# Two layers of attention and gated network on one core: the first layer's bank of sums copied in two halves, by ScalarE and VectorE

## The chip, the core and the metric

The kernel runs on one core of a Trainium2 chip. The time is the device time of one execution in microseconds, and the lower the better. Everything is computed in float32. A core has TensorE (PE in the profile; PEld is its weight load), VectorE (DVE), ScalarE (ACT), GpSimd (POOL) and SyncE (SP, which here only starts DMA transfers). Each engine works through a queue of its own in order. TensorE writes its products into banks of 128 partitions x 512 numbers; ScalarE and VectorE read them from there into the large on-chip memory, and from there DMA transfers take them.

## The reference

Two layers over 2048 tokens of 128 numbers. Each is `x = x + s * silu(f)`, where s is an attention of the normalised x and f a second network of it. The change lies in the attention of the first layer, which has no softmax: a query's weights are the rectified scores, divided by their sum.

```python
def kernel_func(q, k):
    scores = jnp.einsum('bhqd,bhkd->bhqk', q, k) / jnp.sqrt(jnp.asarray(HD, q.dtype))
    w = jax.nn.relu(scores)
    return w / (jnp.sum(w, axis=-1, keepdims=True) + KERN_EPS)
...
attn = kernel_func(q, k)
out = jnp.einsum('bhqk,bhkd->bhqd', attn, v)
out = out.transpose(0, 2, 1, 3).reshape(Bx, Sx, D)
out = out @ w_out + b_out
y = x + out
mu = jnp.mean(y, axis=-1, keepdims=True)
var = jnp.var(y, axis=-1, keepdims=True)
return (y - mu) * jax.lax.rsqrt(var + LN_EPS) * gamma + beta
```

It has 16 heads of 8 numbers and all 2048 keys for each query. The first layer's second network (the routed block) picks 255 tokens by a score, runs a small transformer block on them and puts them back. The second layer has a causal softmax attention of 16 heads of 64 and a gated network; nothing of it is changed.

## The kernel before

`relu_attention` is written as 256 steps. A step n stands for a quarter of the queries (qc, 512 of them), a group of four heads (g) and a block of 128 keys (kb): qc = n // 64, g = n // 16 % 4, kb = n % 16. So 16 steps make a group, and there are 16 groups.

`scores(n)` issues four matmuls (L994), one for each head of the group, each into one of six banks that are used in turn (tag "s"). Each result is rectified and scaled into a tile `rt` by ScalarE (L1002) or by VectorE (L1004). `Work.lesser` (L191) chooses: it keeps a running count of booked time for both engines and gives the piece to the one whose count would be lower. Other pieces that are put on either engine are booked with `work.add`.

`products(m, r)` runs two steps behind the scores: four matmuls (L1010, eight instructions in the profile) multiply the rectified scores with the values. They add up over a group's 16 steps in one bank, `acc`, in which head j has the partitions 32j to 32j + 8 (eight numbers and the sum of the weights). The first step of a group starts the bank afresh.

After the 16th step of a group `group_out` (L1017) copies all 128 x 512 numbers of `acc` into a tile `part` (L1026), one of two in turn, and books 0.6 for ScalarE. Then five DMA transfers take the sums (L1028) and the four heads' rows (L1031) out of `part`. When a quarter of the queries has its four groups, `gated` (L1033) divides, multiplies by the output weights, normalises and applies the gate; it is cut into pieces by `yield`.

PE, ScalarE and VectorE follow the written order. In the main loop (L1143) a step issues: the scores and their rectifiers of step n; a `later` left over from the step before; the products of step n - 2 and, where that was a group's last, `group_out`; then one piece of other work (the routed block's, the second network's weights, or `gated`'s); and at some steps DMA loads of keys and queries. So on ScalarE the copy stands behind the rectifiers of step n, and before the other work of step n and the rectifiers of step n + 1. On PE the scores of step n + 1 stand between the last products of one group and the first of the next, which have to wait until the bank has been copied.

The tile framework sets the waits between the engines: an instruction waits for what it reads, and for those that still use what it overwrites.

Of the kernel before, what the change touches and what calls it, by code (L numbers as in the profile page):

```python
# [16 lines left out]
AF = mybir.ActivationFunctionType  # L17
ALU = mybir.AluOpType
# [88 lines left out]
def layer0(ctx, tc, a, small, ident, xin, xsrc, xn1T, row_load, second):  # L107
# [33 lines left out]
    for n, bit in (("k", 2), ("q", 1)):  # L141
# [30 lines left out]
        row_load, (b_out, gamma, beta, xin),  # L172
    )
    relu_attention(
        tc, work, at, aw, end, dram, small, ps, ident, (w_q, w_k, w_qa, w_ka, w_v), lows, w_out, xin, xne,
        xnT, g0, xn1T, routed, (ends, steps, block), second,
# [589 lines left out]
def relu_attention(  # L766
# [3 lines left out]
    nc = tc.nc  # L770
    scale = 1.0 / math.sqrt(HD0)
# [11 lines left out]
    def bank(shape, tag="x"):  # L783
        return ps.tile(shape, F32, tag=tag, bufs=NS if tag == "s" else 1, name="t")
# [26 lines left out]
    def query_tile(qc, g):  # L811
        t = qTs[qc, g] = aw.tile([P, 512], F32R, tag="qT", bufs=3, name=f"qT_{qc}_{g}")
        return t
# [26 lines left out]
    def group(parts, order, g, dst):  # L840

        for n, x in enumerate(order):
            nc.sync.dma_start(out=dst.bitcast(F32)[n::4, :], in_=parts[x][32 * g : 32 * g + 32, :])
# [4 lines left out]
    def key_group(parts, i, g):  # L848
        group(parts, OF_K, g, kT[:, g, 512 * i : 512 * i + 512])
# [135 lines left out]
    acc = bank([P, 512], "acc")  # L985
    nc.vector.memset(acc, 0.0)

    def scores(n):
        qc, g, kb = n // 64, n // 16 % 4, n % 16
        r = []  # L990
        for j in range(4):
            rows = slice(32 * j, 32 * j + 32)
            t = bank([P, 512], "s")
            nc.tensor.matmul(  # L994
                t, kT[rows, g, kb * P : (kb + 1) * P], qTs[qc, g][rows, :],
                start=True, stop=True,
            )
            rt = aw.tile([P, 512], F32, tag="relu", bufs=12, name="rt")
            r.append((rt, t))
        for rt, t in r:  # L1000
            if work.lesser(512):
                nc.scalar.activation(rt, t, AF.Relu, scale=scale)  # L1002
            else:
                nc.vector.tensor_scalar(rt, t, scale, 0.0, ALU.mult, ALU.max)  # L1004
        return [rt for rt, _ in r]

    def products(n, r):
        g, kb = n // 16 % 4, n % 16
        for j in range(4):
            nc.tensor.matmul(  # L1010
                acc[32 * j : 32 * j + HD0 + 1, :], va[:, kb, 4 * g + j, :], r[j],
                start=(kb == 0), stop=(kb == NC - 1),
            )
# [3 lines left out]
    def group_out(qc, g):  # L1017

        if g == 0:
            got[qc] = [  # L1020
                end.tile([P, 512], F32, tag="on", bufs=3, name=f"on_{qc}"),
                small.tile([P, 64], F32, tag="sums", name=f"sums_{qc}"),
            ]
        on, sums = got[qc]
        part = end.tile([P, 512], F32, tag="part", bufs=2, name="part")
        nc.scalar.copy(part, acc)  # L1026
        work.add(a=0.6)
        nc.sync.dma_start(out=sums[32 * g : 32 * g + 32, :], in_=part[HD0::32, :])  # L1028
        for j in range(4):
            r0 = HD0 * (4 * g + j)  # L1030
            nc.sync.dma_start(out=on[r0 : r0 + HD0, :], in_=part[32 * j : 32 * j + HD0, :])  # L1031
# [94 lines left out]
    def others():  # L1126
        yield from routed
        block.close()
        yield from second.ffn_weights(
            ends.enter_context(tc.tile_pool(name="l1_f", bufs=1, side="right")), work  # L1130
        )
        for qc in range(NQ):
            while qc not in ready:
                yield
            yield from gated(qc)

    ends, steps, block = pools
    ready, held, other, later = set(), [], others(), None
# [4 lines left out]
    for n in range(n_steps + 2):  # L1143
        if n == 16:
            first.close()
        if n < n_steps:
            held.append((n, scores(n)))
        if later:
            later()
            later = None  # L1150
        if n >= 2:
            m, r = held.pop(0)
            products(m, r)
            if m % 16 == 15:
                group_out(m // 64, m // 16 % 4)
        if n in due:
            f, *args = due[n]
            later = f(*args)
        else:
            next(other)  # L1160
        if n in read:
            i, g = read[n]
            key_group(key_rows[i], i, g)
        if n == 11 or (n > 16 and n % 16 == 8 and n + 8 < n_steps):
            m = 16 if n == 11 else n + 8
            qc, g = m // 64, m // 16 % 4
            group(asked[qc], OF_Q, g, query_tile(qc, g))

        if n >= 2 and (n - 2) % 64 == 6 and n > 64:
            ready.add((n - 2) // 64 - 1)  # L1170
# [4 lines left out]
    early = second.early()  # L1175
# [785 lines left out]
```

## Time and profile before

| what | us |
|---|---|
| three runs: lowest, median, highest | 1429.67, 1430.36, 1430.63 |
| the profiled execution, its own time | 1430.62 |
| its span, first instruction to last | 1428.8 |
| the first layer's 256 steps, first products at 18.2 to last at 471.5 | 453 |
| copies of the bank (L1026), 16 of 605 ns | 9.7 |
| rectifiers on ScalarE (L1002), 595 of 606 ns | 315.3 |
| rectifiers on VectorE (L1004), 429 of 684 ns | 276.8 |
| scores on TensorE (L994), 1024 matmuls, time in which any of them runs | 155.9 |
| products on TensorE (L1010), 2048 instructions, time in which any of them runs | 267.4 |

In the stretch from 300 to 400 us TensorE is busy for 98.8 us, VectorE for 84.2 and ScalarE for 83.2; the granted clock of TensorE is 1.00.

How to read the profile's lines. A group of instructions gives the line of the kernel, the engine, the operation, result <- operands by the program's names, the shapes and the count; then the busy time in us, the mean ns of one; then the idle time of the engine just before them and what ended it. `t` is the name that the profile gives to every bank of the first layer, `acc` among them. A line of a timeline gives the start in us from the span's start, the duration in us, and the same names; instructions of one kind that follow each other are drawn together (x8), and the bracket is the idle time of the engine before the first.

### The profile page before, as it was taken

Reading aid. Unit: us, or ns where it says so; the run is one execution under the profiler, and the core shown is the slowest. Engines: PE = TensorE matmul, PEld = TensorE weight load, DVE = VectorE, ACT = ScalarE, POOL = GpSimd, SP = SyncE. Lnnn points to the kernel's source line nnn. Section 1 sums busy time; section 2 is a strip of 40 time slices with the busy share of each in tenths; the row PEclk is TensorE's granted clock in tenths of the full one; section 3 lists DMA queues with packets and bytes.
Section 4 is the critical chain, followed back from the end, with each engine's and each line's share of the span. In section 5 each row is a group of like instructions: output and inputs, shape, how many; then the busy total and the mean of one; then the engine's idle time right before and its main releaser. Section 6 shows DMA issues by size and latency. Waiting matters only on the chain.

```text
span 1428.8 us, 26989 instructions
## 1 busy us (share of the span) xinstructions
PE 1394.9 (98%) x10112; PEld 850.7 (60%) x10112; DVE 1061.3 (74%) x1930; ACT 953.1 (67%) x2054; POOL 307.5 (22%) x414
## 2 busy tenths in 40 slices
PE   8999999999999999999999999999999999999997
PEld 4222332322222477777777777777777777777775
DVE  7688788788888486668668678668768768777775
ACT  5588877788888566666557556566566656656563
POOL 3001000150000131322323232242242233242210
PEclk9999999999999999999999999999999999999999
DMA  3632001101000310111111101111011111111110
GB/s 95 170 78 63 12 13 36 47 27 44 19 20 5 101 38 23 31 31 45 31 28 33 45 16 46 31 31 45 17 45 37 25 31 46 31 31 31 30 38 16
DMA packets 44082, 56.48 MB, mean 40 GB/s; under 512 B 11696, under 2 KB 26416, under 8 KB 43952
## 3 DMA queue, kind: packets, MB, share of 16 engines
q1 hardware_dynamic: 43568, 53.70, 14.7%
q8 instruction: 80, 1.31, 0.4%
q0 software_dynamic: 384, 1.05, 0.3%
q14 instruction: 50, 0.41, 0.1%
HBM read 27.74 MB, written 8.35 MB: 25 GB/s over the span
## 4 chain that ended last, share of the span: by engine, by line
PE 62%; ACT 1%; DVE 1%; issue 0%; DVEq 0%; ACTq 0%
PE t L1520 18%; PE z L1570 18%; PE t L1791 16%; PE m L1671 2%; PE m L1473 2%; PE m L1458 2%; PE m L1423 2%; ACT p L1554 1%; PE m L1352 0%; ACT pt L1798 0%; PE m L1370 0%; DVE tops L1541 0%; DVE zs L1654 0%; DVE res L1689 0%; ACT L1361 0%
## 5 line engine op out<-in xcount | busy, mean ns | idle before, releaser
L1541 DVE TENSOR_REDUCE tops<-t 128x1 f32<-128x1024 f32 (+4 forms) x320 | 334.5, 1062 | 94.7 <-PE t L1520 88.1
L1002 ACT ACTIVATE rt<-t 128x512 f32<-128x512 f32 x595 | 315.3, 606 | 67.8 <-PE t L994 66.5
L1798 ACT COPY pt<-t 128x512 f32<-128x512 f32 (+3 forms) x359 | 163.4, 519 | 262.1 <-PE t L1791 260.9
L1554 ACT ACTIVATE p<-t,tops 128x1024 f32<-128x1024 f32 (+7 forms) x384 | 330.9, 882 | 1.3 <-DVE tops L1541 1.1
L1004 DVE TENSOR_SCALAR rt<-t 128x512 f32<-128x512 f32 x429 | 276.8, 684 | 64.4 <-PE t L994 59.9
L1520 PE MATMUL t<-k,q 128*128 128x512 f32 (+4 forms) x1280 | 312.9, 387 | 3.7 <-ACT p L1554 3.7
L1791 PE MATMUL t<-ident,p 128*128 128x128 f32 x2176 | 270.0, 275 | 2.9 <-ACT x L1444 1.4
L1010 PE MATMUL t<-rt,va 128*9 128x512 f32 x2048 | 267.4, 595 | 4.7 <-ACT part L1026 4.7
L1570 PE MATMUL z<-pt,v 128*64 128x256 f32 (+1 forms) x2304 | 268.4, 374 | 0.5 <-ACT zs L1805 0.5
L1520 PEld LDWEIGHTS t<-k,q 128*128 128x128 f32 x1280 | 217.9, 189 | 77.0 <-issue 32.2
L1791 PEld LDWEIGHTS t<-ident,p 128*128 128x128 f32 x2176 | 243.5, 141 | 25.4 <-ACT pt L1798 5.7
L1570 PEld LDWEIGHTS z<-pt,v 128*64 128x64 f32 x2304 | 152.1, 137 | 86.6 <-issue 22.8
L994 PEld LDWEIGHTS t<-qT,kT 32*128 32x128 f32 x1024 | 65.3, 182 | 181.5 <-ACT rt L1002 99.1
L1798 DVE COPY pt<-t 128x512 f32<-128x512 f32 (+3 forms) x289 | 163.6, 605 | 3.9 <-PE z L1570 2.0
L994 PE MATMUL t<-qT,kT 32*128 32x512 f32 x1024 | 155.9, 496 | 2.8 <-DMA kT<-spread 1.3
L1446 POOL CAST q<-x 64x512 fp32r<-64x512 f32 x60 | 36.5, 609 | 454.5 <-ACT x L1444 452.8
L1540 DVE TENSOR_TENSOR t<-t,mask_q 128x128 f32<-128x128 f32 (+1 forms) x192 | 64.7, 337 | 74.9 <-PE t L1520 68.5
L1554 ACT ACTIVATION_READ_ACCUMULATOR p<-t,tops 128x1 f32 x384 | 84.3, 220 | 0.0
L1448 POOL TENSOR_TENSOR k<-x,k 64x512 fp32r<-64x512 f32 x60 | 76.4, 1273 | 4.6
L1448 POOL TENSOR_TENSOR q<-x,q 64x512 fp32r<-64x512 f32 x60 | 76.2, 1270 | 4.6
L1010 PEld LDWEIGHTS t<-rt,va 128*9 128x9 f32 x2048 | 30.8, 89 | 69.2 <-issue 60.2
L1446 POOL CAST k<-x 64x512 fp32r<-64x512 f32 x60 | 38.3, 639 | 128.6 <-ACT x L1444 126.8
(330 smaller groups left out, 938.1 us busy)
## 6 DMA issues: line engine op xcount, KB each, us to landing
q<-q SPq DMA_DIRECT2D x64, 256.0 KB
wide<-rows SPq DMA_DIRECT2D x90, 128.0 KB
qT<-spread SPq DMA_DIRECT2D x60, 64.0 KB
kT<-spread SPq DMA_DIRECT2D x48, 64.0 KB
spread<-high SPq DMA_DIRECT2D x8, 256.0 KB
spread<-low SPq DMA_DIRECT2D x8, 256.0 KB
rows<-xne SPq DMA_DIRECT2D x1, 1048.0 KB
back<-nothing SPq DMA_DIRECT2D x4, 256.0 KB
```

The costliest lines, as they stand in the source:

```text
L994: nc.tensor.matmul(t, kT[rows, g, kb * P : (kb + 1) * P], qTs[qc, g][rows, :], start=True, stop=True,)
L1002: nc.scalar.activation(rt, t, AF.Relu, scale=scale)
L1004: nc.vector.tensor_scalar(rt, t, scale, 0.0, ALU.mult, ALU.max)
L1010: nc.tensor.matmul(acc[32 * j : 32 * j + HD0 + 1, :], va[:, kb, 4 * g + j, :], r[j], start=(kb == 0), stop=(kb == NC - 1),)
L1446: nc.gpsimd.tensor_copy(high, x[half(e), :])
L1448: nc.gpsimd.tensor_tensor(low, x[half(e), :], high, ALU.subtract)
L1520: nc.tensor.matmul(flat[:, at_x : at_x + y - x], q[:, part, c4 * P : (c4 + 1) * P], k[:, x:y], start=(part == 0), stop=(part == 1),)
L1541: nc.vector.tensor_reduce(M[pr, c // 4][:, h, c % 4, es], x, axes, ALU.max, negate=True)
L1554: nc.scalar.activation(dst, x, AF.Exp, bias=M[pr, c // 4][:, h, c % 4, e : e + 1], accum_out=Z[pr, c // 4][:, h, c % 4, e : e + 1],)
L1570: nc.tensor.matmul(l1.z[half(e), slot, lo:2, :], V[pr, h][:, kb, half(e)], pts[e][:, kb, lo:2, :], start=(kb == 0), stop=(kb >= n0 - 1), s ...
L1791: nc.tensor.transpose(t[:, k + b, :], x[lo + b], ident)
L1798: copy(dst, t)
```

## The change

`group_out` copies the columns 0 to 255 of the bank by ScalarE and the columns 256 to 511 by VectorE, one after the other in the written order, and books 0.4 for each. `scores` returns, besides its tiles, a function that rectifies those of the four results that it hasn't rectified itself; the loop calls it after the products. How many it rectifies itself is given by the loop, and it is 4 in both branches.

```diff
-    def scores(n):
+    def scores(n, early=4):
...
-        for rt, t in r:
-            if work.lesser(512):
-                nc.scalar.activation(rt, t, AF.Relu, scale=scale)
-            else:
-                nc.vector.tensor_scalar(rt, t, scale, 0.0, ALU.mult, ALU.max)
-        return [rt for rt, _ in r]
+
+        def rectified(some):
+            for rt, t in some:
+                if work.lesser(512):
+                    nc.scalar.activation(rt, t, AF.Relu, scale=scale)
+                else:
+                    nc.vector.tensor_scalar(rt, t, scale, 0.0, ALU.mult, ALU.max)
+
+        rectified(r[:early])
+        return [rt for rt, _ in r], lambda: rectified(r[early:])
...
         part = end.tile([P, 512], F32, tag="part", bufs=2, name="part")
-        nc.scalar.copy(part, acc)
-        work.add(a=0.6)
+
+        nc.scalar.copy(part[:, :256], acc[:, :256])
+        nc.vector.tensor_copy(part[:, 256:], acc[:, 256:])
+        work.add(a=0.4, d=0.4)
...
+        rest = None
         if n < n_steps:
-            held.append((n, scores(n)))
+
+            rows, rest = scores(n, 4 if n % 16 == 1 and n > 16 else 4)
+            held.append((n, rows))
...
+        if rest:
+            rest()
```

## The prediction

> **What bounds the kernel now.** I read the page first (busy shares, then the costliest groups), then the copy's own line, then the timeline at one end of a group, then looked for a place where ScalarE and VectorE already read one bank.
>
> ```profile
> PE 1394.9 (98%) x10112; PEld 850.7 (60%) x10112; DVE 1061.3 (74%) x1930; ACT 953.1 (67%) x2054; POOL 307.5 (22%) x414
> ...
> L1010 PE MATMUL t<-rt,va 128*9 128x512 f32 x2048 | 267.4, 595 | 4.7 <-ACT part L1026 4.7
> ```
>
> TensorE is busy for 98% of the span. Where it stands idle in the products of the first layer, the only releaser named is the copy of the bank, 4.7 us in all. The copy's own line says how often:
>
> ```profile
> L1026 ACT COPY part<-t x16: 585/600/651, 60.7 to 472.2; 128x512 f32<-128x512 f32 x16
> ...
>   PEld t L1010: 9.0, 14
>   PE t L1010: 4.7, 12
> ```
>
> So 12 of the 16 copies leave TensorE idle, 0.27 to 0.48 us each. The timeline shows how, at the end of the seventh group:
>
> ```profile
> 243.77 1.05 PE L1010 MATMUL t<-rt,va 128*9 128x512 f32 x8
> ...
> 243.96 2.60 DVE L1004 TENSOR_SCALAR rt<-t 128x512 f32<-128x512 f32 x4
> ...
> 244.74 0.50 PE L994 MATMUL t<-qT,kT 32*128 32x512 f32 x4
> 244.88 0.58 ACT L1026 COPY part<-t 128x512 f32<-128x512 f32 x1
> ...
> 245.52 1.04 PE L1010 MATMUL t<-rt,va 128*9 128x512 f32 x8 [0.27 <-ACT part L1026]
> ...
> 246.93 1.05 PE L1010 MATMUL t<-rt,va 128*9 128x512 f32 x8
> ```
>
> The group's last products end near 244.81, the copy runs from 244.88 to 245.46, and the next group's first products start 0.06 later. Between them TensorE has only the next step's scores (0.50). The step over the end takes 245.52 - 243.77 = 1.75 us, the one after it 246.93 - 245.52 = 1.41, which is the shortest step between neighbours until the last two. From 300 to 400 us TensorE is busy for 98.8 of 100 us, so time lost at an end isn't won back.
>
> **The change, part by part.**
>
> The copy. One ScalarE copy of 128x512 becomes a ScalarE and a VectorE copy of 128x256 each. Both forms stand in the trace, PSUM to SBUF:
>
> ```profile
> L1805 ACT COPY zs<-z 128x256 f32<-128x256 f32 x96 | 35.5, 380 | 6.6 <-PE z L1570 6.3
> ...
> L1798 DVE COPY pt<-t 128x256 f32<-128x256 f32 x17 | 7.0, 414 | 0.4 <-PE t L1791 0.4
> ...
> L1026 ACT COPY part<-t 128x512 f32<-128x512 f32 x16 | 9.7, 605 | 1.8 <-PE t L1010 1.7
> ```
>
> Half the columns cost 63% of the time on ScalarE, and the two halves together 0.794 us. What the change is worth hangs on whether they run at once. Their columns are apart, but the bank is one. The trace has such a case: L1437 reads the two partition halves of a bank on ScalarE, and L1439 reads the same halves on VectorE. L1439's first instruction needs only L1437's first result.
>
> ```profile
> 494.80 1.38 ACT L1437 ACTIVATE k<-m,b_k 64x512 fp32r<-64x512 f32 x2 [1.12 <-PE m L1423]
> ...
> 496.21 1.51 DVE L1439 SCALAR_TENSOR_TENSOR k<-m,b_k,k 64x512 fp32r<-64x512 f32 x2 [1.51 <-ACT k L1437]
> ```
>
> The first of the two activations (0.68 each) is done at 495.48, and VectorE, idle since 494.70, starts only at 496.21, 0.03 after the second. The two query cases do the same (ScalarE ends at 490.98 and 501.24, VectorE starts at 491.07 and 501.27). So the program lets the engines into one bank one after the other, even for reads of separate parts, with a hop of 0.03 to 0.09 us. I take it that the VectorE half waits for the ScalarE half.
>
> The Trainium skill, PSUM — Partial Sum Buffer, section "PSUM bank collisions raise a hardware error", gives a rule that speaks against this change: two different engines may not touch one bank in the same 32 partitions at once, two reads of disjoint columns included. All 128 partitions are copied here, so by the rule the halves have to be put in order; without it each end would be worth what the side-by-side rival below says. The rows of L1437 and L1439 agree on the order, though they read different partitions; no run here shows a collision.
>
> From the start of the copy to the next products it is now 0.605 + 0.05 = 0.655 us (0.64 to 0.66 at the ends that stall). In series it becomes 0.380 + 0.06 (hop, 0.03 to 0.09) + 0.414 + 0.05 = 0.904 (0.87 to 0.93): **0.25 us more**, bounds 0.22 to 0.28. The start itself doesn't move: it is set by the group's last products, or by the ScalarE rectifiers ahead in its queue. VectorE's own rectifiers of the step end at most 0.37 after the start (seventh group), so VectorE is free when the hop comes.
>
> Counted by ends, from the timeline around each: 12 stalls grow by 0.25, 3.0 in all. At 92.04 the products start 0.70 after the copy's start without idle time: they move to 0.90, +0.2. At 183.45 they start at 0.84 because transposes of the routed block lie before them: +0.06. At 60.71 they start at 1.30: nothing, its cover is a 1.1 us pair of router matmuls. After the last copy (472.24) the second layer's first matmul waits for the same bank: between 0 and +0.25, since later a load of b_k holds that stretch up for 3.9 us on ScalarE; I take 0.15. Sum **3.4 us**.
>
> The new wait on VectorE. Queued behind the half are the routed block's or the gating's instructions of that step and then the next step's rectifiers, which release the banks for the scores after. In the clean case they start at 0.83 to 0.84 after the copy's start in place of 0.39; the scores that need them come at 1.6 + 0.25, so 1.5 is early enough. It is dearer where VectorE now runs ahead:
>
> ```profile
> 349.02 0.26 DVE L1098 BATCH_NORM_STATS2 ln_st<-y 128x6 f32<-128x128 f32 x1
> 349.20 0.61 ACT L1026 COPY part<-t 128x512 f32<-128x512 f32 x1
> 349.31 0.18 DVE L1099 BATCH_NORM_AGGREGATE ln_mv<-ln_st 128x2 f32<-128x6 f32 x1
> 349.41 1.27 DVE L1004 TENSOR_SCALAR rt<-t 128x512 f32<-128x512 f32 x2
> ```
>
> Here four statistics (348.60 to 349.49) would start at 350.04, and the next rectifier end near 351.6, while the scores that take its bank come at 350.84 + 0.25: 0.5 us late. At 217 the routed softmax's maximum (L632) moves 0.6 us, and ScalarE's exponentials behind it: up to 0.3. At 119 and 150 what moves is read late enough. So 0 to 0.8 for these, up to 2 if more ends behave so; I take 0.5.
>
> ScalarE is relieved by 0.225 us per end, VectorE loaded by 0.414. ScalarE isn't what the next products wait for any more, so its part buys nothing by itself.
>
> The planner. The copy is booked as 0.4 on each engine in place of 0.6 on ScalarE. A rectifier is booked at 0.603 or 0.683, so one that changes sides moves the balance by 1.286; 0.6 per group moves 0.47 of a rectifier, some 7 of VectorE's 429, to ScalarE. VectorE: +16 x 0.414 - 7 x 0.684 = +1.8 us of busy time; ScalarE: -16 x 0.225 + 7 x 0.606 = +0.6. Neither is the bound on average, but evictions hold scores up in places: the scores' union of 155.9 us over 256 steps is 0.61 each against 0.50 undisturbed, 28 us in all. Reshuffling which engine takes which rectifier can move some of that either way; 5% of it is 1.5 us. I take 0, bounds -1.5 to +1.5.
>
> The rest. The five DMAs of part (issued by SyncE) wait for the later half, 0.25 us later; the reciprocal of the sums comes 6.9 us after the copy at the nearest (479.10 behind 472.24), and the next query loads on that queue seven steps after. The split of the rectifiers into an early and a late list issues nothing: both branches give 4, so the late list is empty. Cost 0.
>
> **Sum.** 3.4 + 0.5 + 0 = 3.9 us. The profiled execution took 1430.62 (span 1428.8 and 1.8 around it), so 1434.5 by its measure; the runs' median is 0.26 lower, 1430.36, so **1434.2 us**, +0.27%. The case's own range is 1431.8 to 1436.9: -0.9 for hop and cover, +0.8 or more for the queue, 1.5 for the planner. About 0.2% (2.9 us) is what a measurement of this kernel can tell from no change: slower begins at 1433.2, faster below 1427.5.
>
> **Rivals.**
>
> *In series, as above*: 0.60. Of this I put 0.48 over the bound and 0.12 under it.
>
> *The halves run side by side* (the edit then does what its words say): 0.08. For it: the columns are disjoint. Against it: L1439. VectorE's rectifiers still come first in its queue and end up to 0.37 after the copy's start, so its half ends between 0.41 (rectifiers done early, six ends) and 0.70 (the ends at 244.88 and 323.13). Against 0.605 now: six ends win 0.2, one 0.13, two lose 0.1, the others stand within 0.05; about 1 us won, **1429.4**.
>
> *The planner pays it back* (the rival on the other side): 0.17. Its place is the steps just after an end: there the 0.6 booked on ScalarE alone now gives VectorE three rectifiers (the ends at 299.25, 374.55, 425.69 and 450.34), some 1.9 us against a step of 1.41. Even bookings give two and two. Each unit of delay that this takes from the scores behind, about 0.25 us per end, cancels the serial copy's; it decides from 3.9 / 16 = 0.24 per end. Against it: the second and third step after these ends already take 1.41 or little more. **1430.4**, with a tail to 1426.5 where it wins twice as much.
>
> *The VectorE queue falls behind* (0.15): work held behind the half piles onto the three-rectifier steps and stalls the scores at most ends, not two. 0.25 more at 16 ends: 3.9 + 4.0, **1438.3**. For it: VectorE loses 0.44 us or more at each end, and a step of 1.41 with two rectifiers (spaced 0.61) wins back only 0.2. Against it: no other VectorE work in most steps after 245 us.
>
> **How the numbers follow.** Slower: 0.48 + 0.15 = 0.63. Same: 0.12 from the series, 0.07 side by side, 0.13 planner = 0.32. Faster: 0.04 planner, 0.01 side by side = 0.05. The range from 1430.0 to 1438.5 leaves out half the planner's case, most of the side-by-side one and part of the falling-behind one, just under 0.2.
>
> **What would show it.** In the changed profile: two copies of 128x256 per end, VectorE's starting 0.03 to 0.09 after ScalarE's ends; the products' idle time rising from 4.7 to about 7.7 us and naming VectorE's half; the step over a clean end at 2.0 instead of 1.75; VectorE idle ahead of its half, with ScalarE's half as releaser. If VectorE's half starts before ScalarE's ends, the order is not there and I am wrong at the root. If the idle time rises by 3 us and the span doesn't, the planner's shift or slack in the scores took it. If the span rises by 8, look at the scores' union (155.9 now).

## The result, and the profile after

The changed kernel takes 1432.63 us (median of 14 runs, 1431.92 to 1434.24) against 1430.32 for the kernel before in the same measurement: the ratio is 1.0015, with a 95% interval from 1.0009 to 1.0022. That is 2.1 us slower, between 1.3 and 3.1. It went the way that was forecast, inside the range, but 1.8 us short of the forecast's 3.9.

The page of the changed kernel, the busy shares and the group of the products:

```profile
PE 1393.0 (97%) x10112; PEld 848.2 (59%) x10112; DVE 1062.8 (74%) x1939; ACT 954.2 (67%) x2061; POOL 307.3 (21%) x414
...
L1014 PE MATMUL t<-rt,va 128*9 128x512 f32 x2048 | 267.3, 595 | 8.3 <-DVE part L1032 7.8
```

The products (now L1014) stand idle for 7.8 us because of the copy, in place of 4.7, and they name VectorE's half (L1032). That half's own line:

```profile
L1032 DVE COPY part<-t x16: 414/425/426, 59.8 to 473.9; 128x256 f32<-128x256 f32 x16
its engine sat idle before it (us, times) until:
  ACT part L1031: 9.2, 10
who waited for it (us, times):
  PEld t L1014: 11.8, 13
  PE t L1014: 7.8, 12
```

9.2 us of VectorE's own idle time end when ScalarE's half (L1031) is done. The timeline at a clean end:

```profile
272.25 1.05 PE L1014 MATMUL t<-rt,va 128*9 128x512 f32 x8
...
273.23 0.51 PE L994 MATMUL t<-qT,kT 32*128 32x512 f32 x4
273.37 0.37 ACT L1031 COPY part<-t 128x256 f32<-128x256 f32 x1
...
273.77 0.42 DVE L1032 COPY part<-t 128x256 f32<-128x256 f32 x1
...
274.25 0.12 PEld L1014 LDWEIGHTS t<-rt,va 128*9 128x9 f32 x8 [0.83 <-issue]
274.25 1.05 PE L1014 MATMUL t<-rt,va 128*9 128x512 f32 x8 [0.51 <-issue]
...
275.66 1.05 PE L1014 MATMUL t<-rt,va 128*9 128x512 f32 x8
```

ScalarE's half, a hop, VectorE's half, then the products, 0.88 us after the copy's start. The step over the end takes 274.25 - 272.25 = 2.00 us where a clean end took 1.75, and the next step is again 1.41. (The idle time is put down to "issue" here, but the products start 0.05 after VectorE's half.)

To see where the time went I split the first layer's 256 steps into the 15 steps that cross an end of a group (from one group's last products to the next group's first) and the steps within a group, and subtracted the profile before. In this execution the 15 steps over the ends are 3.73 us longer, and the steps within groups, from the second group on, 1.09 us shorter. So the ends cost 3.73 us where 3.26 was forecast for these 15, and something gives a part back between them. (Its first products come 1.11 us earlier and the first group's steps are 0.23 shorter, both before any changed step, which is why the span grows by only 1.43.)

### The profile page after: what moved, and what is told of

Its sections match the earlier page's. It is cut to its first block, busy times and chain, and to the rows that moved or that the text cites. A ratio compares the mean times of both kernels' runs of the same rounds, so it can differ in the third digit from the quotient of the medians.

```text
span 1430.3 us, 26982 instructions
## 1 busy us (share of the span) xinstructions
PE 1393.0 (97%) x10112; PEld 848.2 (59%) x10112; DVE 1062.8 (74%) x1939; ACT 954.2 (67%) x2061; POOL 307.3 (21%) x414
## 3 DMA queue, kind: packets, MB, share of 16 engines
q8 instruction: 80, 1.31, 0.4%
## 4 chain that ended last, share of the span: by engine, by line
PE 62%; ACT 1%; DVE 1%; issue 0%; ACTq 0%; DVEq 0%
PE t L1531 18%; PE z L1581 18%; PE t L1802 16%; PE m L1682 2%; PE m L1484 2%; PE m L1469 2%; PE m L1434 2%; ACT p L1565 1%; PE m L1363 0%; ACT pt L1809 0%; PE m L1381 0%; DVE tops L1552 0%; DVE zs L1665 0%; DVE res L1700 0%; ACT L1372 0%
## 5 line engine op out<-in xcount | busy, mean ns | idle before, releaser
L1004 ACT ACTIVATE rt<-t 128x512 f32<-128x512 f32 x605 | 320.4, 607 | 68.5 <-PE t L994 67.2
L1006 DVE TENSOR_SCALAR rt<-t 128x512 f32<-128x512 f32 x419 | 271.0, 684 | 56.7 <-PE t L994 51.2
L1014 PE MATMUL t<-rt,va 128*9 128x512 f32 x2048 | 267.3, 595 | 8.3 <-DVE part L1032 7.8
L1014 PEld LDWEIGHTS t<-rt,va 128*9 128x9 f32 x2048 | 30.6, 88 | 73.1 <-issue 61.3
```

Source lines behind the costliest of these rows:

```text
L1014: nc.tensor.matmul(acc[32 * j : 32 * j + HD0 + 1, :], va[:, kb, 4 * g + j, :], r[j], start=(kb == 0), stop=(kb == NC - 1),)
```

## The experiments

Each kernel was timed beside the kernel before on the same chip: numbers 1 to 4 on one chip, 5 to 8 on a second, 9 to 11 on a third. "Over the ends" and "within" are the two sums just described, from one profiled execution each; the difference in time is worked out from the ratio and its interval. All edits but the eighth's are to the copy in `group_out` of the changed kernel or to the number of early rectifiers.

| kernel | ratio [95%] | difference, us | over the ends, us | within, us |
|---|---|---|---|---|
| the change | 1.0015 [1.0009, 1.0022] | +2.1 [+1.3, +3.1] | +3.73 | -1.09 |
| 1 bookings alone | 0.9992 [0.9982, 1.0002] | -1.1 [-2.6, +0.3] | +0.28 | -0.42 |
| 2 halves, old booking | 1.0022 [1.0013, 1.0030] | +3.1 [+1.9, +4.3] | +3.18 | +0.88 |
| 3 both halves on ScalarE | 1.0005 [0.9996, 1.0014] | +0.7 [-0.6, +2.0] | +0.71 | +0.20 |
| 4 VectorE's half not from the bank | 0.9984 [0.9975, 0.9994] | -2.3 [-3.6, -0.9] | -2.70 | +2.58 |
| 5 VectorE's half first | 1.0015 [1.0006, 1.0024] | +2.1 [+0.9, +3.4] | +2.65 | -0.40 |
| 6 one copy, late rectifiers | 0.9996 [0.9987, 1.0004] | -0.6 [-1.9, +0.6] | -3.01 | +1.26 |
| 7 the change, late rectifiers | 1.0013 [1.0005, 1.0022] | +1.9 [+0.7, +3.1] | +0.14 | +1.35 |
| 8 two banks of sums, five of scores | 1.0160 [1.0146, 1.0173] | +22.9 [+20.9, +24.7] | -5.76 | +27.58 |
| 9 as 6, with the new booking | 0.9999 [0.9990, 1.0008] | -0.1 [-1.4, +1.1] | -2.83 | +3.63 |
| 10 one copy on the planned engine | 0.9998 [0.9990, 1.0007] | -0.3 [-1.4, +1.0] | -0.67 | +2.00 |
| 11 as 10, with late rectifiers | 1.0005 [0.9996, 1.0013] | +0.7 [-0.6, +1.9] | -2.23 | +3.54 |

In the profiles of 4, 7, 9, 10 and 11 TensorE's granted clock fell for a few us near 155 us, and the group there took 1.5 to 2.1 us longer. The last section shows it; it is in their "within", and not in the steps over the ends.

**1. The bookings alone.**

```diff
-        nc.scalar.copy(part[:, :256], acc[:, :256])
-        nc.vector.tensor_copy(part[:, 256:], acc[:, 256:])
+        nc.scalar.copy(part, acc)
         work.add(a=0.4, d=0.4)
```

> One ScalarE copy of 512 columns as before, but booked as 0.4 on each engine, as in the change. If the halves in series are what costs, the bookings alone give between -1.5 and +0.7 us against the kernel before (I expect -0.5), and the products' idle time stays near 4.7 us. If the planner's new placement of the rectifiers is what costs, this kernel alone shows the change's +2.3 us.

The interval holds zero, but it excludes the +2.1 of the change: the planner isn't what costs. The change moves ten rectifiers to ScalarE (605 and 419, from 595 and 429), and so does this kernel. Its steps over single ends differ from before by up to 0.49 us either way (+0.49 at 92 us, +0.45 at 245, -0.45 at 349), because one rectifier more or less on ScalarE stands ahead of the copy (near 245 us three instead of two, so that the copy starts 0.50 us after the group's last products instead of 0.07); the sum is only +0.28. Subtracting this kernel from the change, end by end, leaves 0.22 to 0.31 at twelve of the 15 ends, 0 at two and 0.45 at one (near 217 us, where VectorE is still rectifying and its half starts 0.26 us after ScalarE's ends), 3.45 in all: what the halves cost, whatever the planner does.

**2. The halves with the old booking.**

```diff
-        work.add(a=0.4, d=0.4)
+        work.add(a=0.6)
```

> The two halves of the change, but booked as before (0.6 on ScalarE). If the halves run in series, VectorE's half starts 0.02 to 0.09 us after ScalarE's ends, at every end of a group, the products follow 0.87 to 0.93 us after the copy's start in place of 0.65, and the kernel is 2.7 to 4.5 us slower than before (I expect 3.4). If the planner is what costs, it is within 0.7 us of the kernel before.

All of it as the series has it. Twelve steps over ends are longer by 0.24 to 0.26 us each; the others by 0.01 (at 61 us), 0.14 (at 119, where the copy also starts 0.10 us earlier) and 0.05 (at 184). VectorE's half starts 0.032 or 0.033 us after ScalarE's ends at all 16 ends. The group of the products from this kernel's page:

```profile
L1014 PE MATMUL t<-rt,va 128*9 128x512 f32 x2048 | 267.6, 595 | 7.9 <-DVE part L1032 7.9
```

VectorE's half from the view of its own line, with what it waited for:

```profile
L1032 DVE COPY part<-t x16: 424/425/426, 60.8 to 476.4; 128x256 f32<-128x256 f32 x16
...
  ACT part L1031: 7.9, 13
```

The same idle time as with the new booking, without the planner's part.

**3. Both halves on ScalarE.**

```diff
         nc.scalar.copy(part[:, :256], acc[:, :256])
-        nc.vector.tensor_copy(part[:, 256:], acc[:, 256:])
-        work.add(a=0.4, d=0.4)
+        nc.scalar.copy(part[:, 256:], acc[:, 256:])
+        work.add(a=0.6)
```

> Both halves on ScalarE, one behind the other, booked 0.6 as before: the split without a second engine. ScalarE starts one 512-column instruction 0.48 us after the other, so two halves should overlap and end some 0.65 us after the start in place of 0.605. If the hop and VectorE's duration are what costs: 0.3 to 1.2 us slower than before (I expect 0.7). If cutting the copy in two is what costs, whatever the engine: 2.3 us or more.

The group of the products from this kernel's page:

```profile
L1014 PE MATMUL t<-rt,va 128*9 128x512 f32 x2048 | 267.3, 595 | 5.5 <-ACT part L1032 5.5
```

Idle time 5.5 us instead of 4.7, and 0.06 to 0.08 us more at most ends. Two halves on one engine overlap: the second starts 0.10 to 0.18 us before the first ends. Cutting the copy in two costs about a quarter of what crossing to the other engine costs. The time as a whole can't tell it from no change.

**4. VectorE's half from another tile.** The second half of every group's sums is left out.

```diff
-        nc.vector.tensor_copy(part[:, 256:], acc[:, 256:])
-        work.add(a=0.4, d=0.4)
+        nc.vector.tensor_copy(part[:, 256:], xnT[:, :256])
+        work.add(a=0.6)
```

> ScalarE copies columns 0 to 255 of the bank; VectorE's half is filled from an ordinary tile (xnT) and not from the bank, so the second half of each group's sums is left out of the computation. Booked 0.6 as before. What orders the halves is gone if it was the bank: VectorE's half then starts without regard to ScalarE's, and the products wait for 0.38 + 0.05 us, less than the scores between (0.50): their idle time falls from 4.7 to under 1.5 us and the kernel is 2 to 4 us faster than before (I expect 3). If VectorE's half still starts only behind ScalarE's, the order comes from the tile part or from the written order, not from the bank.

The timeline at the clean end that was shown of the change:

```profile
275.89 0.51 PE L994 MATMUL t<-qT,kT 32*128 32x512 f32 x4
276.08 0.38 ACT L1031 COPY part<-t 128x256 f32<-128x256 f32 x1
276.22 0.28 DVE L1032 COPY part<-xnT 128x256 f32<-128x256 f32 x1
276.42 1.29 DVE L1006 TENSOR_SCALAR rt<-t 128x512 f32<-128x512 f32 x2
276.51 0.12 PEld L1014 LDWEIGHTS t<-rt,va 128*9 128x9 f32 x8 [0.43 <-issue]
276.51 1.05 PE L1014 MATMUL t<-rt,va 128*9 128x512 f32 x8
```

Both halves still write the tile `part`, and in the same written order, yet VectorE no longer waits: it starts 0.2 us or more before ScalarE's half ends at 14 of 16 ends, some of them before ScalarE has even begun, and 0.085 us before at the other two. So the order comes from the shared bank. (`acc` fills its bank, so a wait set for the tile `acc` and one set for the bank can't be told apart here.) Neither half overwrites what the other uses: besides the two kinds of wait named ahead of the prediction, this program has one between two engines that read the same bank. The products start 0.43 after the copy's start and hardly wait (1.8 us left, at ends where ScalarE is late). This is at most what the change could have won with this booking: 2.70 us at the ends.

**5. VectorE's half first.**

```diff
-        nc.scalar.copy(part[:, :256], acc[:, :256])
         nc.vector.tensor_copy(part[:, 256:], acc[:, 256:])
-        work.add(a=0.4, d=0.4)
+        nc.scalar.copy(part[:, :256], acc[:, :256])
+        work.add(a=0.6)
```

> VectorE's half is written first and ScalarE's half behind it, booked 0.6 on ScalarE as before. If the bank lets in one engine after the other in the written order, ScalarE's half starts behind VectorE's, and the end depends on when VectorE has done its rectifiers: where it has done them before the group's last products end (near 119, 349, 425 us) the halves hide under ScalarE's rectifiers and the step over the end gets 0.2 us shorter; where it has not (near 244, 323, 450) it gets 0.4 to 0.55 longer. Sum about +3.0 us (2 to 4) against the kernel before. If instead the extra cost comes with VectorE's share whatever the order, every end is longer by 0.25 us as with ScalarE's half first.

The timeline at two ends, the first where VectorE was free early, the second where it was not:

```profile
118.02 0.42 DVE L1031 COPY part<-t 128x256 f32<-128x256 f32 x1 [0.26 <-PE t L1014]
...
118.51 0.39 ACT L1032 COPY part<-t 128x256 f32<-128x256 f32 x1
...
118.96 0.62 PE L1014 MATMUL t<-rt,va 128*9 128x512 f32 x4 [0.27 <-ACT part L1032]
```

```profile
245.23 0.42 DVE L1031 COPY part<-t 128x256 f32<-128x256 f32 x1
...
245.68 0.37 ACT L1032 COPY part<-t 128x256 f32<-128x256 f32 x1 [0.68 <-DVE part L1031]
...
246.11 0.62 PE L1014 MATMUL t<-rt,va 128*9 128x512 f32 x4 [0.80 <-ACT part L1032]
```

Now ScalarE waits for VectorE (0.68 us at the second). The steps near 119, 349 and 425 us are 0.21, 0.21 and 0.19 shorter than before, those near 244, 323 and 450 are 0.53, 0.52 and 0.41 longer, as the series in written order has it. A share of VectorE's that costs 0.25 wherever it stands falls here. The sum, 2.65 us, lies within the 2 to 4 expected.

**6. One copy, late rectifiers.**

```diff
-        nc.scalar.copy(part[:, :256], acc[:, :256])
-        nc.vector.tensor_copy(part[:, 256:], acc[:, 256:])
-        work.add(a=0.4, d=0.4)
+        nc.scalar.copy(part, acc)
+        work.add(a=0.6)
...
-            rows, rest = scores(n, 4 if n % 16 == 1 and n > 16 else 4)
+            rows, rest = scores(n, 2 if n % 16 == 1 and n > 16 else 4)
```

> One ScalarE copy of 512 columns, booked 0.6 as before; but at the last step of a group only two of the four scores are rectified before the products, and the other two after the copy (the change's function of late rectifiers, now used). In the kernel before, the copy starts late at some eight ends, 0.27 to 0.84 us after the group's last products end, because ScalarE still rectifies. If the copy's start is worth as much as its length, these ends win up to 3.3 us together, the step over them falls toward 1.75, and the kernel is 1.5 to 3 us faster than before. If the late rectifiers hold up the scores behind them, this is given back: within 1 us of before.

The steps over the ends win 3.01 us, as worked out, and the products' idle time for the copy falls to 1.7 us. But the steps within the groups give 1.26 back, 0.37 of it in one step near 154 us and 0.58 in one near 218, and the whole is within 0.2% of before; the gain of 1.5 to 3 us isn't shown.

**7. The change with late rectifiers.**

```diff
-            rows, rest = scores(n, 4 if n % 16 == 1 and n > 16 else 4)
+            rows, rest = scores(n, 2 if n % 16 == 1 and n > 16 else 4)
```

> The change itself, with two of the four rectifiers of a group's last step put behind the two halves. If the halves in series are a fixed price per end, this kernel stands 3 to 4 us above the one with a single copy and late rectifiers, less some 0.5 for the bookings. If VectorE's half had been held by the rectifiers ahead of it rather than by ScalarE's half, its wait is gone here and it is faster than the kernel before.

Over the ends it stands 3.15 us above number 6 (0.14 against -3.01), and the products wait 4.6 us for VectorE's half. Against number 9, which has the change's booking too, it is 2.97. The fixed price again, with little ahead of the halves that could have held them up: at 14 of the 16 ends ScalarE's half starts within 0.15 us of the group's last products and VectorE's 0.03 after ScalarE's ends (the two others are near 92 us, where ScalarE's half starts 0.27 later, and near 217, where VectorE's starts 0.14 after ScalarE's).

**8. Two banks of sums, five banks of scores.** This one edits the banks as well.

```diff
-NS = 6
+NS = 5
...
-    acc = bank([P, 512], "acc")
-    nc.vector.memset(acc, 0.0)
+    accs = [bank([P, 512], f"acc{i}") for i in range(2)]
+    for acc in accs:
+        nc.vector.memset(acc, 0.0)
...
-                acc[32 * j : 32 * j + HD0 + 1, :], va[:, kb, 4 * g + j, :], r[j],
+                accs[n // 16 % 2][32 * j : 32 * j + HD0 + 1, :], va[:, kb, 4 * g + j, :], r[j],
...
+        nc.scalar.copy(part, accs[g % 2])
+        work.add(a=0.6)
```

> The groups use two banks of sums in turn, and the scores have five banks instead of six, since eight is all there is. One ScalarE copy, booked 0.6. The products of the next group no longer wait for the copy: their idle time for it falls from 4.7 us to 0. What it costs is a bank of the scores: a score then waits for the rectifier five scores back instead of six, and the scores' busy union (155.9 us) rises. If the wait for the bank is the dearer, the kernel is 2 to 4 us faster than before; if the scores' bank is, it is 3 us or more slower.

The groups of the products and of the scores in this kernel:

```profile
L1015 PE MATMUL t<-rt,va 128*9 128x512 f32 x2048 | 267.3, 595 | 0.0
...
L995 PE MATMUL t<-qT,kT 32*128 32x512 f32 x1024 | 181.3, 496 | 6.9 <-DVE p L626 4.0 <-ACT rt L1005 1.7 <-DMA kT<-spread 0.9
```

The wait is gone (0.0), and the kernel is 22.9 us slower: the scores' union grows from 155.9 to 181.3 us, because they wait for their banks. The timeline shows one such step, in which the four scores take 1.45 us instead of 0.50:

```profile
264.91 1.45 PE L995 MATMUL t<-qT,kT 32*128 32x512 f32 x4
265.38 0.18 PEld L995 LDWEIGHTS t<-qT,kT 32*128 32x128 f32 x1 [0.29 <-ACT rt L1005]
...
265.87 0.18 PEld L995 LDWEIGHTS t<-qT,kT 32*128 32x128 f32 x1 [0.31 <-ACT rt L1005]
```

The weights of the third and the fourth wait for ScalarE's rectifiers, which read the banks. The Trainium skill, Perfetto Trace Analysis, section "Matmuls", advises that matmul groups should go round through different banks so that one's eviction overlaps the next one's matmuls. That is what this kernel does for the sums, and its idle time shows that it works; but the bank came from the scores, where it was worth far more.

**9, 10, 11. Other ways to start the copy early.** Number 9 is number 6 with the booking of 0.4 on each engine. Numbers 10 and 11 replace the two halves by one planned copy, 11 with late rectifiers as well:

```diff
-        nc.scalar.copy(part[:, :256], acc[:, :256])
-        nc.vector.tensor_copy(part[:, 256:], acc[:, 256:])
-        work.add(a=0.4, d=0.4)
+        work.copy(part, acc, 512)
```

> One ScalarE copy of 512 columns, booked 0.4 on each engine, and two of the four rectifiers of a group's last step put behind it. The steps over the ends won 3.0 us with late rectifiers under the old booking, and the rest of the steps gave half of it back. If what was given back came from the late pieces being booked onto VectorE after the copy's 0.6, the even booking gives back less: 1.5 to 3 us faster than before. If it belongs to the late rectifiers themselves, the kernel is within 1 us of before.

> One copy of 512 columns on whichever engine has the lower booked count, no late rectifiers. One engine per bank, so no hop and no second duration. Where the planner's count says what the engines really have ahead, the copy goes to VectorE at the ends at which ScalarE is still rectifying (near 119, 349, 425 us) and starts 0.4 us earlier: 1 to 3 us faster than before. Where the count doesn't, some copies of 0.69 us take the place of 0.605: within 1 us of before, or up to 1 us slower.

> The planned copy of one engine and the late rectifiers together. The copy should start with the group's last products at every end, and the step over an end be 1.75 (ScalarE) or 1.83 (VectorE) us throughout. If the start is what these ends still have to give, 1.5 to 3 us faster than before; if the planned engine and the late rectifiers only win the same ends twice, the same as the better of the two alone.

None brings the gain hoped for. Each wins at the ends (0.67 to 2.83 us), and none is told apart from the kernel before; their steps within groups are 2.0 to 3.6 us longer in the profiled executions, of which the group with the lower clock near 155 us holds 1.5 to 2.1. What makes up the rest, 0.5 to 1.6 us, is open. No kernel here that computes everything is shown to beat the kernel before.

## Why the prediction was right, and where it was off

**The copy in series: right, in mechanism and size.** The forecast's root was that the two halves follow one another because they share a bank, read from L1437 and L1439. Number 5 shows that the written order decides who waits, number 4 that the wait goes when VectorE reads elsewhere. The Trainium skill's rule on the PSUM bank (PSUM — Partial Sum Buffer, "PSUM bank collisions raise a hardware error") gives the reason why such reads are kept apart; that they are kept apart is measured here, a collision is not, and two unordered reads of one bank weren't tried. The 15 ends were put at 3.0 + 0.2 + 0.06 = 3.26 us; number 2 measured 3.18, and the time +3.1. That the sum fits so well is in part luck: the hop is 0.03 us, the low end of 0.03 to 0.09, VectorE's half is 0.425, not 0.414, and the end near 119 us gave 0.14 where 0.25 was counted.

**The work held behind VectorE's half: not borne out.** It was put at 0.5 us, from two places. At 217 us number 2's third step of the group (the step over the end is the first) is 0.29 longer than before (2.35 against 2.06), within the 0.3 given for the softmax chain. But in number 4, where VectorE's half doesn't wait, the same step is 0.32 longer, so that the wait is the cause isn't shown; and in the change itself the step isn't longer (2.00). At 349 nothing was lost, where 0.5 was forecast. The timeline of number 2 there:

```profile
351.38 1.13 ACT L1004 ACTIVATE rt<-t 128x512 f32<-128x512 f32 x2
351.56 0.42 DVE L1032 COPY part<-t 128x256 f32<-128x256 f32 x1 [0.93 <-ACT part L1031]
351.90 0.28 DVE L1104 BATCH_NORM_STATS2 ln_st<-y 128x6 f32<-128x128 f32 x1
...
352.71 1.25 DVE L1006 TENSOR_SCALAR rt<-t 128x512 f32<-128x512 f32 x2
...
353.01 0.50 PE L994 MATMUL t<-qT,kT 32*128 32x512 f32 x4
```

VectorE's rectifiers do start late (352.71), but ScalarE had done two of the four by 352.51, and only two banks are needed for the scores at 353.01, which run undisturbed in 0.50 us. I had given the first bank to VectorE without looking at who had it.

**ScalarE's relief: put at nothing, worth 0.45 us at one end.** The prediction says that ScalarE's shorter part "buys nothing by itself". Near 151 us it does. After the copy and the next rectifiers ScalarE goes on there to the routed softmax: it loads a table (ACT_TABLE_LOAD, 1.28 us), takes exponentials (L637), and only then comes to the rectifiers for which the scores of the group's third step wait. The kernel before, then the changed kernel:

```profile
151.28 1.05 PE L1010 MATMUL t<-rt,va 128*9 128x512 f32 x8 [0.47 <-ACT part L1026]
...
152.72 1.28 ACT L637 ACT_TABLE_LOAD   x1
...
155.63 1.06 ACT L1002 ACTIVATE rt<-t 128x512 f32<-128x512 f32 x2
...
156.25 0.49 PE L994 MATMUL t<-qT,kT 32*128 32x512 f32 x1 [0.41 <-ACT rt L1002]
```

```profile
150.83 1.05 PE L1014 MATMUL t<-rt,va 128*9 128x512 f32 x8 [0.72 <-DVE part L1032]
...
151.82 1.28 ACT L637 ACT_TABLE_LOAD   x1
...
154.72 1.06 ACT L1004 ACTIVATE rt<-t 128x512 f32<-128x512 f32 x2
...
155.35 0.50 PE L994 MATMUL t<-qT,kT 32*128 32x512 f32 x2 [0.54 <-ACT rt L1004]
```

Counted from the group's first products, the load starts after 0.99 us instead of 1.45. The third step takes 2.68 us instead of 3.13, in number 2 as well; in numbers 1, 3 and 5, where ScalarE copies the whole bank, copies both halves or comes second, it stays within 0.02 of before. So in this group the halves cost 0.24 over the end and win 0.45 behind it: 0.21 us faster, about what ScalarE is relieved of (0.22).

**The planner: its size is not shown.** It was taken as 0, with bounds of -1.5 to +1.5 us. The bookings alone measured -1.1 us, with an interval (-2.6 to +0.3) that holds zero; and the intervals of the change and of number 2 (2.1 and 3.1) overlap, so their difference is no measure of it either. The trace shows that the new placement moves single steps within the groups by up to 0.58 us either way, alike in the change and in number 1 (at 66, 74 and 395 us by -0.24, +0.58 and +0.49 in the change, by -0.24, +0.57 and +0.48 in number 1). In number 1 they add up to -0.42, and with +0.28 over the ends to -0.14; most of the rest of its span's 1.08 us (0.68) lies ahead of its first products, where no booking of a copy has been made. The forecast also held the start of the copy to be fixed; with the rectifiers ahead of it, it moves by up to 0.49. Seven rectifiers were to move, ten did.

**The last end: about right.** The second layer's first matmul comes 0.24 us later behind the copy (0.88 instead of 0.64). The span grows by 1.43 us while the first layer's last products come 1.31 later, so some 0.12 of it remains; 0.15 was taken.

**The rivals.** Side by side falls with number 2: VectorE's half never starts before ScalarE's ends. The planner paying all of it back falls, since the change is slower by an interval that excludes zero; that it paid a part isn't shown. The VectorE queue falling behind, 0.25 us more at every end, falls with the even 0.25 at twelve ends of number 2 and with the shorter steps between them in the change.

**The sum.** The sum 3.4 + 0.5 + 0 came out, in the change's profile, as 3.73 + 0.12 at the ends (3.45 and 0.12 from the halves, 0.28 from the bookings) and -1.09 between them (-0.45 from ScalarE's relief, -0.42 as in number 1, -0.22 open): 2.8 us, which the interval of the time, 1.3 to 3.1, holds. So the ends were put a little too low, and what lies between them, +0.5, had the wrong sign. With 1432.63 us the change also stays under the 1433.2 from which the prediction counts a kernel as slower: by that line the result is "same", to which it gave 0.32, and not "slower", to which it gave 0.63.

## What to carry to other kernels

In this program a bank is read by one engine after the other: splitting its copy between ScalarE and VectorE puts two short instructions and a hop (0.39 + 0.03 + 0.42 us) in place of one (0.60), and cost 0.25 us at most ends. Before sharing a piece of work between engines, look in the trace for a place where they already share that resource and see who waits for whom, and follow the engine that is relieved as well as the one that is loaded. Where a group waits for its bank, the start of the copy was worth as much as its length (3.0 us for late rectifiers against 2.7 for half a copy, at the ends), but the steps between gave part of it back, so such an edit is judged by the whole time.

## What the runs showed of the hardware

Half the columns cost 62 to 65% of the time on ScalarE (medians of 0.372 to 0.391 against 0.60 us) and 62% on VectorE (0.425 against 0.69); two halves on ScalarE overlap and end only 0.06 to 0.08 us after one whole copy would. The hop from one engine's end to the other's start was 0.032 or 0.033 us from ScalarE to VectorE (number 2, all 16 ends), and 0.033 or 0.034 from VectorE to ScalarE (number 5, 15 of 16).

TensorE's granted clock fell in the middle of some executions. Three windows of number 7, then one of the kernel before (columns: busy time and count of PE, PEld, DVE, ACT and POOL, then the clock, the DMA share and GB/s):

```profile
148.00:160.00 12.00, 10.98 (x72) 3.27 (x64) 9.64 (x15) 10.90 (x23) 0.00 (x0) 0.86 0.04 7
...
155.00:158.50 3.50, 3.50 (x18) 0.55 (x20) 1.75 (x3) 3.50 (x9) 0.00 (x0) 0.51 0.01 2
158.50:162.00 3.50, 3.50 (x32) 1.34 (x24) 2.81 (x6) 1.77 (x4) 0.00 (x0) 1.00 0.00 0
```

```profile
148.00:160.00 12.00, 11.02 (x84) 4.12 (x82) 9.68 (x15) 10.80 (x22) 0.00 (x0) 1.00 0.06 13
```

The 0.86 is a mean: the clock was about half for 3.5 us and full around it, and 18 matmuls ran in those 3.5 us where 32 ran in the next. In five of 13 profiled executions (numbers 4, 7, 9, 10 and 11) the clock was 0.86 to 0.90 in the window from 148 to 160 us, and the 15 steps within the group that begins there took 1.5 to 2.1 us longer than before; in the other eight it was 1.00, and in six of the seven that can be compared they stayed within 0.5 us (the seventh is number 8, which is slower in every group). Numbers 2, 4, 5, 6, 9, 10 and 11 show 0.50 to 0.58 from 18 to 21 us too, in the first group, which the sums leave out. Such a loss is as much as this change: single executions of such kernels can't be compared without the clock of each stretch, and a sum over places where the clock is full tells more. What lowers the clock there is open.
